# Layer 0's neighbour sums for seven row blocks from two float32r pieces, and an 8-bit mask read directly

## The chip, the cores and the metric

The kernel runs on one core of a Trainium2 chip. The metric is the device time of one execution in microseconds, as the median over repeated executions. The engines are PE (TensorE, matmuls), DVE (VectorE), ACT (ScalarE), POOL (GpSimd, here mostly the gathers) and SP (SyncE, which issues the other transfers).

## The reference

Four graph layers follow each other on a matrix x of 3327 rows and 512 columns, each with a residual and a layer norm, over one sparse 0/1 adjacency. The change lies in layer 0, a graph attention layer with 8 heads of 64 columns:

```python
Wh = einsum('nd,hdo->hno', x, W)
f1 = einsum('hno,ho->hn', Wh, a1);  f2 = einsum('hno,ho->hn', Wh, a2)
e  = leaky_relu(f1[:, :, None] + f2[:, None, :], 0.2)
e  = where(adj > 0, e, -9e15)
h  = einsum('hnm,hmo->hno', softmax(e), Wh)
x  = layernorm(x + elu(h))
```

Layer 1 sums masked neighbours and multiplies by dense weights, layer 2 does so over the first 64 neighbours of a row, layer 3 is another attention layer with 4 heads.

## The kernel before

The 3327 rows are 26 blocks of 128. A first stage, `structure`, reads the adjacency block by block and makes, for every block but block 0, a list of its edges (`EdgeList`). Density falls with the row number, so the lists get shorter: in chunks of 128 edges they hold 19, 15, 13, 11, 10, 9 for blocks 1 to 6, then 9, 8, 8, 8, 7, 7, 7 for blocks 7 to 13, and 7 down to 5 for blocks 14 to 25. Block 0 is dense and is not done by a list.

`projection` writes the rows of Wh with their scores, 8 heads of 66 columns (528 in all), into a table in DRAM. Then, per block, `groups` cuts the list into groups of at most `GROUP = 4` chunks, and `Gat.group` does a group in stages (each `yield` ends one). Line numbers are those of the profile:

- POOL gathers 528-column rows of the table into the ring tile `gt` (line 973); ACT computes `far` (1206), DVE from it the selector `ds` (1210).
- PE brings the rows' own scores to the edges (1218) and turns the selector (1224). DVE adds the scores (1228, 1229), ACT takes two exponentials (1230, 1231) and copies the turned selector out of PSUM into `sel` (1233).
- DVE multiplies the gathered rows by their weights in place (1238).
- PE adds `sel`-transposed times rows into two accumulators of 264 columns, in float32 (1249), chunk by chunk.

When a block's last chunk is in, `layer0_end` divides by head (1361 to 1365, ACT does 8 divisions), does ELU and layer norm (1375 to 1378, 789, 791, and on POOL the root, 799 and 800; `nm` 843 and the scaled row 844), turns the result (769, 772) and multiplies it by two weights of layer 1 (784), whose results go to DRAM in two pieces (1546, 1547) or as they are (1554). For this, steps of an earlier block stand between the steps of the groups.

Block 0 is done densely beside the last seven lists: `open_dense` makes a factor per head, and `dense` takes one block of 128 table rows after another (`gd`, loaded on SP), scales them by ACT (1315, eight heads), makes a weight matrix of 8 x 128 columns by DVE (1316, 1317), which is masked by block 0's adjacency, and adds the product (1324). That mask is kept as `row0` in 8-bit floats; ACT first copies it into a float32 tile `mk` with two buffers (1306), which line 1317 reads.

Up to and including layer 0 the instructions stand in the order that the scheduler of the language gives them when the kernel is built; from layer 1 on they stand as written. Every engine runs its queue in order. Tiles come from pools with a fixed number of buffers: a write into a tile waits until the last reader of the earlier tile in that buffer has ended.

Of the kernel before, what the change touches and what calls it, by code (L numbers as in the profile page):

```python
# [8 lines left out]
F32 = mybir.dt.float32  # L9
BF16 = mybir.dt.bfloat16  # L10
FP8 = mybir.dt.float8e4
F32R = mybir.dt.float32r
# [5 lines left out]
AF = mybir.ActivationFunctionType  # L18
# [5 lines left out]
P = 128  # L24
# [509 lines left out]
GROUP = 4  # L534
# [6 lines left out]

FIRST = 1
DENSE = 7
RING = 22 * 528
MORE = 3072
RANGE = 60.0
# [29 lines left out]
class Ring:  # L576
# [20 lines left out]
    def done(self):  # L597

        self.live.pop(0)
# [28 lines left out]
def sparse_path(ctx, tc, flag_i, x, adj, l0_w, l0_a1, l0_a2, l1_w_self, l1_b_self, l1_w_nb, l1_b_nb,  # L628
# [13 lines left out]
    nc = tc.nc  # L642
    N, D = x.shape
    NB = (N + P - 1) // P
# [10 lines left out]
    def pool_in(lay, name, bufs=1, **kw):  # L655
        return lay.enter_context(tc.tile_pool(name=name, bufs=bufs, reuse_waits="tile", **kw))
# [17 lines left out]
    chunks_of = [sum(l.L for l in ls) for ls in lists]  # L674
# [67 lines left out]
    H0, _, OUT0 = l0_w.shape  # L742
# [207 lines left out]
                                                   ALU.is_gt, ALU.mult)  # L950
            yield k

    def groups(ring, blocks=range(NB)):


        for b in blocks:
            at = 0
            for l in lists[b]:
                c0 = 0
                while c0 < l.L:  # L960
                    left = l.L - c0
                    g = -(-left // -(-left // GROUP))
                    if ring.ahead() < g:
                        g = ring.ahead()
                    yield b, l, c0, g, at
                    c0 += g
                    at += g
# [26 lines left out]
    class Gat:  # L994
# [197 lines left out]
        def group(self, item, pools, accs, done, sall=None):  # L1192

            b, l, c0, g, at = item
            ring, sp, pacc, pone = pools
            H, OUT, M = self.H, self.OUT, self.M
            hh = H // 2
            G = gather(ring, self.table, l, c0, g)

            m = l.places(c0 + g - 1)  # L1200
            for p0 in range(m, P, 32):
                nc.scalar.copy(G[p0:p0 + 32, g - 1].rearrange("p (h m) -> p h m", m=M)[:, :, OUT:],
                               zeros[p0:p0 + 32, :2 * H].rearrange("p (h s) -> p h s", s=2))

            far = sp.tile([P, GROUP * P], I16, name="far")
            nc.scalar.activation(far[:, :g * P], place[:, c0 * P:(c0 + g) * P], AF.Abs, bias=l.nmid, scale=2.0)
            yield
            have = kept(sall, b, at, g)
            ds = sp.tile([P, GROUP * P], BF16, name="ds")
            nc.vector.tensor_scalar(ds[:, :g * P], far[:, :g * P], dgs[:, l.at:l.at + 1], None, ALU.is_lt)  # L1210
            yield

            pg = pone.tile([P, 512], F32, name="pg")
            pe = pg[:, :GROUP * 2 * H].rearrange("p (c s h) -> p c s h", c=GROUP, s=2)
            w = pg[:, GROUP * 2 * H:GROUP * 3 * H].rearrange("p (c h) -> p c h", c=GROUP)
            for c in range(g):
                for k in range(3):
                    nc.tensor.matmul(pe[:, c], ds[:, c * P:(c + 1) * P], self.own[:, k, :, b],
                                     start=k == 0, stop=k == 2)
            S = sp.tile([P, GROUP, P], F32, name="sel")  # L1220
            if have is None:
                turned = pg[:, 256:].bitcast(BF16)
                for c in range(g):
                    nc.tensor.transpose(turned[:, c * P:(c + 1) * P], ds[:, c * P:(c + 1) * P], ident16)
            yield
            sc = sp.tile([P, GROUP, 2, H], F32, name="sc")
            Gh = G.rearrange("p c (h m) -> p c h m", m=M)
            nc.vector.tensor_tensor(sc[:, :g], pe[:, :g], Gh[:, :, :, OUT:].rearrange("p c h s -> p c s h"), ALU.add)
            nc.vector.tensor_tensor(sc[:, :g, 0], sc[:, :g, 0], sc[:, :g, 1], ALU.max)
            nc.scalar.activation(w[:, :g], sc[:, :g, 0], AF.Exp)  # L1230
            nc.scalar.activation(Gh[:, :, :, OUT], sc[:, :g, 0], AF.Exp)  # L1231
            if have is None:
                nc.scalar.copy(S[:, :g], turned[:, :g * P].rearrange("p (c i) -> p c i", i=P))  # L1233
            else:
                nc.scalar.activation(S[:, :g], have, AF.Identity)
            yield
            Gc = G.rearrange("p c (h m) -> p (c h) m", m=M)
            nc.vector.tensor_mul(Gc[:, :, :OUT], Gc[:, :, :OUT],  # L1238
                                 w[:, :g].rearrange("p c (h o) -> p (c h) o", o=1).to_broadcast([P, g * H, OUT]))
            yield  # L1240
            while self.held[self.turn] if at == 0 else b not in accs:
                yield
            if at == 0:
                accs[b] = self.sums(pacc, self.turn)
                self.turn ^= not self.pinned
            for c in range(g):
                m = l.places(c0 + c)
                for s in range(2):
                    nc.tensor.matmul(accs[b][s], S[:m, c, :], G[:m, c, s * hh * M:(s + 1) * hh * M],  # L1249
                                     start=at + c == 0, stop=at + c == chunks_of[b] - 1)  # L1250
            ring.done()
            if at + g == chunks_of[b]:
                done(b, accs.pop(b))

        def sums(self, pacc, turn):

# [37 lines left out]
        def dense(self, j, pool, ps, pacc, done):  # L1294
# [7 lines left out]
            gd, wt = self.gd[j % 3], self.wt[j % 2]  # L1302
            for p0, p1 in rows_of(j):
                nc.sync.dma_start(gd[p0:p1], self.table[2 + j * P + p0:2 + j * P + p1, :])
            mask = pool.tile([P, P], F32, name="mk", bufs=2)
            nc.scalar.activation(mask, row0[:, j, :], AF.Identity)
            yield
            g = gd.rearrange("p (h m) -> p h m", m=M)
            fs = pool.tile([P, 2, H], F32, name="fs", bufs=2)
# [4 lines left out]
            for h in range(H):  # L1314
                nc.scalar.activation(g[:m, h, :OUT], g[:m, h, :OUT], AF.Identity, scale=g[:m, h, OUT:OUT + 1])
            nc.vector.tensor_tensor(wt[:m], self.up[:m], fs[:m, 1, :, None].to_broadcast([m, H, P]), ALU.max)
            nc.vector.tensor_mul(wt[:m], wt[:m], mask[:m, None, :].to_broadcast([m, H, P]))
            yield

            def out(h):  # L1320
# [238 lines left out]
    def transposed_weights():  # L1559

        n = len(raws) - 2
        jobs = [(src, o, k) for src, o in ((l2_w_nb, wn2), (l2_w_line, wl2)) for k in range(DC)]

        def fetch(i):
            src, _, k = jobs[i]
            nc.sync.dma_start(raws[i % n], src[k * P:(k + 1) * P, :])

        for i in range(n):
            fetch(i)
        yield  # L1570
        for i, (_, o, k) in enumerate(jobs):
            yield
            pt = ps.tile([P, DC, P], F32, name="pt", tag="tr")
            for c in range(DC):
                nc.tensor.transpose(pt[:, c, :], raws[i % n][:, c * P:(c + 1) * P], ident)
            nc.scalar.copy(o[:, :, k * P:(k + 1) * P], pt)
            if i + n < len(jobs):
                fetch(i + n)

    w2lay, dlay = ExitStack(), ExitStack()  # L1580
    def feed():

        left = list(range(NB))
        blocks = [b for b in order if b]
        for n, b in enumerate(blocks):
            if n == len(blocks) - DENSE - 2:
                assert wn2 is not None
                dp = pool_in(dlay, "l0d")
                work.add(g0.open_dense(fin, ps, pools[2], dp.tile([P, H0 * P], F32, name="up"),
                                       *[raws[-1 - k] for k in range(2)],  # L1590
                                       *[dp.tile([P, H0 * g0.M], F32, name=f"gd{k}") for k in range(3)]))
            for item in groups(pools[0], (b,)):
                yield item
                for _ in range(2):
                    if left and n >= len(blocks) - DENSE:
                        yield left.pop(0)
        yield from left

    for k, item in enumerate(feed()):
        if isinstance(item, int):  # L1600
            work.add(g0.dense(item, fin, ps, pools[2], layer0))
        else:
            while ready < order.index(item[0]):
                more()
            work.add(g0.group(item, pools, accs, layer0))
        work.step()
        more(2)
        if ready == NB - 1 and wn2 is None:
            listlay.close()
            aside = pool_in(ctx, "s_more")  # L1610
            wp = pool_in(w2lay, "l2w")
            wn2 = wp.tile([P, DC, D], F32, name="wn2")
            wl2 = wp.tile([P, DC, D], F32, name="wl2")
            places = aside.tile([P, MORE], F32, name="raw", tag="aside")
            raws = [places[:, k * D:(k + 1) * D] for k in range(2)]
            raws += [places[:, (k + 1) * H0 * P:(k + 2) * H0 * P] for k in range(2)]
            work.add(transposed_weights())
    ps = Banks(ps, acc0=pools[2])
    ps.shared = dict(po="acc0")
# [376 lines left out]
```

## Time and profile before

| | |
|---|---|
| median of 8 runs | 1724.51 us (1721.97 to 1731.35) |
| the profiled execution | 1719.89 us, span 1718.2 us |
| PE, PE's weight loads | busy 1515.5 us (88%), 1010.1 us (59%) |
| DVE, ACT, POOL | 1194.8 us (70%), 821.1 us (48%), 858.7 us (50%) |
| granted PE clock, mean | 0.951 |
| line 1249, layer 0 (rows `gt`) | 804 matmuls from 226.7 to 670.0 us, 386 ns median each |

A recorded matmul's duration holds its way through the array, which the next one overlaps; what a stream of them costs is read from the distance of their starts. A float32 matmul of the kernel stands in the trace as two instructions. The busy share of the whole span says little, since the stages have different bounds: the text reads each stage by itself.

### The profile page before, as it was taken

What the parts mean: (1) busy time and instruction counts of PE and PEld (TensorE: products, weight loads), DVE (VectorE), ACT (ScalarE), POOL (GpSimd) and SP (SyncE); (2) the same over time, 40 slices, a digit from 0 to 9 for tenths busy, and PEclk for the clock granted to TensorE, in tenths of its full rate; (3) what the DMA queues carried; (4) which work ended last, traced back from release to release, by engine and by line L of the source; (5) the groups of instructions that cost most, each with busy time, mean ns of one, the idle gap of its engine ahead of it and who ended that gap; (6) DMA issues with size and microseconds to landing.
All of it is one profiled execution on the core that took longest, in us unless ns stands there. A gap on an engine that the chain in (4) does not pass through costs nothing.

```text
span 1718.2 us, 24775 instructions
## 1 busy us (share of the span) xinstructions
PE 1515.5 (88%) x7729; PEld 1010.1 (59%) x7729; DVE 1194.8 (70%) x2887; ACT 821.1 (48%) x2728; POOL 858.7 (50%) x936
## 2 busy tenths in 40 slices
PE   5899868999999998899999998768999987698774
PEld 4666656666666675355555554324666765577653
DVE  8987889975578795046566676566666545788986
ACT  4887856675557685121212111203444443465664
POOL 2000076655545300566555653177777706777770
PEclk9899978999999999889999999999999998899997
DMA  8787688766555531899999998288999916777772
GB/s 288 231 290 249 195 301 283 233 211 196 175 162 167 166 97 44 296 376 344 297 349 330 350 395 290 88 294 285 306 321 316 325 39 170 213 230 224 229 223 71
DMA packets 127073, 414.45 MB, mean 241 GB/s; under 512 B 23299, under 2 KB 24835, under 8 KB 126932
## 3 DMA queue, kind: packets, MB, share of 16 engines
q0 software_dynamic: 78128, 293.23, 52.7%
q1 hardware_dynamic: 48804, 119.55, 20.0%
q8 instruction: 63, 1.03, 0.2%
q14 instruction: 78, 0.64, 0.1%
HBM read 364.40 MB, written 48.30 MB: 240 GB/s over the span
## 4 chain that ended last, share of the span: by engine, by line
PE 42%; DVE 7%; DMA 7%; ACT 5%; issue 3%; POOL 2%; DVEq 0%; POOLq 0%; ACTq 0%
PE po L784 14%; PE acc L1681 11%; PE acc L1249 5%; PE po L1010 5%; DMA gl<-t_d,idx 3%; PE pt L769 2%; DMA gm<-t_d,idx 2%; PE acc L1175 1%; DMA gk<-t_d,idx 1%; POOL gl L973 1%; DVE gl L1238 1%; ACT h L1365 1%; DVE st L789 1%; PE acct L1324 1%; PE acc L1757 1%
## 5 line engine op out<-in xcount | busy, mean ns | idle before, releaser
L973 POOL DMA_INDIRECT gl<-t_d,idx x334 | 330.7, 990 | 197.1 <-issue 137.5
L973 POOL DMA_INDIRECT gt<-t_d,idx x201 | 201.2, 1001 | 333.4 <-DVE g0fall L832 201.3
L973 POOL DMA_INDIRECT gm<-t_d,idx x159 | 158.5, 997 | 115.8 <-PE acc L1681 62.5
L1249 PE MATMUL acc<-gt,sel 128*128 128x264 f32 (+3 forms) x804 | 207.1, 405 | 1.5 <-issue 1.4
L1249 PE MATMUL acc<-gl,sel 128*128 128x260 f32 (+3 forms) x684 | 176.6, 410 | 32.8 <-issue 24.0
L784 PE MATMUL po<-wn,xt 128*128 128x512 f32 x416 | 195.1, 612 | 9.7 <-ACT xt L772 5.7
L1249 PEld LDWEIGHTS acc<-gt,sel 128*128 128x128 f32 (+3 forms) x804 | 151.5, 197 | 39.3 <-issue 14.9
L1249 PEld LDWEIGHTS acc<-gl,sel 128*128 128x128 f32 (+3 forms) x684 | 132.3, 201 | 59.2 <-issue 29.4
L784 PEld LDWEIGHTS po<-wn,xt 128*128 128x128 f32 x416 | 79.0, 196 | 93.9 <-issue 77.0
L1681 PE MATMUL acc<-gm,selr 128*128 128x512 f32 (+2 forms) x360 | 119.8, 464 | 9.4 <-DMA gm<-t_d,idx 6.7
L1238 DVE TENSOR_TENSOR gt<-gt,pg 128x1536 f32<-128x1536 f32 (+3 forms) x63 | 116.5, 1849 | 14.1 <-ACT sel L1233 13.8
L1010 PE MATMUL po<-gt,xt 128*128 128x268 f32 x416 | 109.3, 410 | 8.9 <-ACT xt L776 5.7
L772 ACT COPY xt<-pt 128x512 f32<-128x512 f32 x81 | 47.4, 592 | 135.6 <-PE pt L769 125.8
L892 DVE MAX8 cand<-val 128x8 f32<-128x464 uint16 (+32 forms) x184 | 106.1, 619 | 0.0
L769 PE MATMUL pt<-s_ident,xres 128*128 128x128 f32 x500 | 77.4, 282 | 30.2 <-DMA xres<-in_x_dram 16.3
L1238 DVE TENSOR_TENSOR gl<-gl,pg 128x1536 f32<-128x1536 f32 (+3 forms) x53 | 98.2, 1852 | 2.2 <-ACT gl L1231 2.0
L1010 PE MATMUL po<-w,xt 128*128 128x262 f32 x416 | 98.6, 390 | 0.5 <-ACT xt L776 0.5
L784 PE MATMUL po<-wx,xt 128*128 128x512 f32 x208 | 95.4, 604 | 0.4 <-DVE t L1547 0.4
L1681 PEld LDWEIGHTS acc<-gm,selr 128*128 128x128 f32 (+2 forms) x360 | 67.5, 201 | 47.1 <-issue 18.5
L1010 PEld LDWEIGHTS po<-gt,xt 128*128 128x128 f32 x416 | 77.9, 196 | 28.5 <-ACT xt L776 7.8
L868 ACT ACTIVATE m<-ab 128x1664 bf16<-128x1664 int32 x50 | 81.1, 1624 | 27.1 <-DMA ab<-in_adj_dram 18.8
L784 PE MATMUL po<-wl,xt 128*128 128x512 f32 x208 | 93.1, 593 | 0.0
(334 smaller groups left out, 3063.8 us busy)
## 6 DMA issues: line engine op xcount, KB each, us to landing
ab<-in_adj_dram SPq DMA_DIRECT2D x25, 832.0 KB, 6.8
ab<-in_adj_dram SPq DMA_DIRECT2D x25, 831.5 KB, 6.2
t_d<-t SPq DMA_DIRECT2D x25, 512.0 KB, 3.2
gm<-t_d POOLq DMA_DIRECT2D x20, 512.0 KB, 9.5
t_d<-t SPq DMA_DIRECT2D x25, 384.0 KB, 6.7
t_d<-tg SPq DMA_DIRECT2D x25, 264.0 KB, 4.9
gd<-t_d SPq DMA_DIRECT2D x25, 264.0 KB, 3.3
t_d<-tg SPq DMA_DIRECT2D x25, 260.0 KB, 5.2
```

What stands on the lines that cost most here:

```text
L769: nc.tensor.transpose(pt[:, c, :], src[:, c * P:(c + 1) * P], ident)
L772: nc.scalar.copy(xt, pt)
L784: nc.tensor.matmul(po, xt[:, c, :], w[:, c], start=c == 0, stop=c == DC - 1)
L789: nc.vector.bn_stats(st, y)
L868: nc.scalar.activation(m, ab[s], AF.Sign, accum_out=half[:, s, b:b + 1])
L892: nc.vector.max(out=cand[:, s, :], in_=val[:, cuts[s]:cuts[s + 1]])
L973: nc.gpsimd.indirect_dma_start(out=t[:m, c, :], out_offset=None, in_=table[:, :], in_offset=bass.IndirectOffsetOnAxis(ap=l.idx[:m, c0 + c: ...
L1010: nc.tensor.matmul(pw[s], xt[:, c, :], self.w[:, c, s, :], start=c == 0, stop=c == DC - 1)
L1175: nc.tensor.matmul(self.acc[h // hh][:, h % hh, :], wt[:m, h, :], G[:m, h, :], start=False, stop=False)
L1238: nc.vector.tensor_mul(Gc[:, :, :OUT], Gc[:, :, :OUT], w[:, :g].rearrange("p c (h o) -> p (c h) o", o=1).to_broadcast([P, g * H, OUT]))
L1249: nc.tensor.matmul(accs[b][s], S[:m, c, :], G[:m, c, s * hh * M:(s + 1) * hh * M], start=at + c == 0, stop=at + c == chunks_of[b] - 1)
L1681: nc.tensor.matmul(accs[b], chosen, parts[:, k * D:(k + 1) * D], start=at + c + k == 0, stop=k == top and at + c == n - 1)
```

## The change

In blocks 7 to 13 of layer 0 (`PARTED`) a group has at most 3 chunks. After the product of line 1238, ACT copies the group's rows into a float32r tile `hi`, and DVE subtracts that from the rows into a second one, `lo`; both are halves of one tile `hl` with a single buffer. `sel` is float32r in these blocks. PE then adds `sel` times `hi` and `sel` times `lo` instead of one float32 product. The pool that held the dense block's `up` and three `gd` tiles is opened earlier, when the structure stage ends, and has one buffer, which first holds `hl` and then, as `room0`, those four. Line 1317 reads `row0` itself; `mk` and its copy are gone.

```diff
+PARTED = range(7, 14)
+THREE = 3
...
-    def groups(ring, blocks=range(NB)):
+    def groups(ring, blocks=range(NB), most=lambda b: GROUP):
...
-                    g = -(-left // -(-left // GROUP))
+                    g = -(-left // -(-left // most(b)))
...
-            S = sp.tile([P, GROUP, P], F32, name="sel")
+            split = self.k == 0 and b in PARTED
+            S = sp.tile([P, GROUP, P], F32R if split else F32, name="sel" + "r" * split, tag="sel")
...
-            yield
+            if split:
+                hi, lo = self.parts()
+                nc.scalar.copy(hi[:, :g], G)
+            yield
+            if split:
+                nc.vector.tensor_sub(lo[:, :g], G, hi[:, :g].bitcast(F32))
...
+                parts = (hi, lo) if split else (G,)
                 for s in range(2):
-                    nc.tensor.matmul(accs[b][s], S[:m, c, :], G[:m, c, s * hh * M:(s + 1) * hh * M],
-                                     start=at + c == 0, stop=at + c == chunks_of[b] - 1)
+                    for k, part in enumerate(parts):
+                        nc.tensor.matmul(accs[b][s], S[:m, c, :], part[:m, c, s * hh * M:(s + 1) * hh * M],
+                                         start=at + c + k == 0,
+                                         stop=at + c == chunks_of[b] - 1 and k == len(parts) - 1)
...
+        def parts(self):
+            hl = self.dp.tile([P, 2, THREE, self.H * self.M], F32R, name="hl", tag="d")
+            return hl[:, 0], hl[:, 1]
...
-            mask = pool.tile([P, P], F32, name="mk", bufs=2)
-            nc.scalar.activation(mask, row0[:, j, :], AF.Identity)
...
-            nc.vector.tensor_mul(wt[:m], wt[:m], mask[:m, None, :].to_broadcast([m, H, P]))
+            nc.vector.tensor_mul(wt[:m], wt[:m], row0[:m, j, None, :].to_broadcast([m, H, P]))
...
-                dp = pool_in(dlay, "l0d")
-                work.add(g0.open_dense(fin, ps, pools[2], dp.tile([P, H0 * P], F32, name="up"),
-                                       *[raws[-1 - k] for k in range(2)],
-                                       *[dp.tile([P, H0 * g0.M], F32, name=f"gd{k}") for k in range(3)]))
-            for item in groups(pools[0], (b,)):
+                room0 = g0.dp.tile([P, 2 * THREE * H0 * g0.M], F32, name="room0", tag="d")
+                gds = [room0[:, H0 * P + k * H0 * g0.M:][:, :H0 * g0.M] for k in range(3)]
+                work.add(g0.open_dense(fin, ps, pools[2], room0[:, :H0 * P], *[raws[-1 - k] for k in range(2)],
+                                       *gds))
+            for item in groups(pools[0], (b,), lambda b: THREE if b in PARTED else GROUP):
...
+            g0.dp = pool_in(dlay, "l0d")
             work.add(transposed_weights())
```

## The prediction

> **What bounds the kernel now.** I read the page first (its slices show PE at 9 tenths in slices 9 to 12 while DVE and ACT stand at 4 to 7), then the order of the work on PE to find where blocks 7 to 13 lie. Line 1249 runs 4 recorded matmuls a chunk (two column halves, each float32 product in two passes), blocks 1 to 6 have 77 chunks and blocks 7 to 13 have 54, so the blocks of the change are its instructions 309 to 524; counted through the stages, they stand at 362 to 472 us. The busy times by stage:
>
> ```profile
> core 0: us, PE busy (x) PEld busy (x) DVE busy (x) ACT busy (x) POOL busy (x), PEclk, DMA share, GB/s
> 362.00:472.00 110.00, 109.02 (x604) 74.44 (x603) 66.00 (x148) 65.65 (x197) 59.23 (x72) 1.00 0.64 195
> 215.00:362.00 147.00, 121.96 (x834) 89.10 (x831) 134.63 (x371) 90.18 (x257) 100.63 (x104) 0.88 0.81 262
> 520.00:600.00 80.00, 74.94 (x459) 56.17 (x458) 62.49 (x109) 58.37 (x221) 38.63 (x39) 1.00 0.54 166
> 600.00:660.00 60.00, 57.81 (x396) 46.15 (x396) 53.87 (x95) 49.08 (x200) 5.77 (x6) 1.00 0.29 92
> ```
>
> From 362 to 472 PE is the bound, with 1 us idle in 110, and DVE and ACT have 44 us free each. In the stage before, DVE is the bound (92%). So the matmuls that the change shortens are on the path. PE's order of time inside it:
>
> ```profile
> 435.11 3.73 PE L1249 MATMUL acc<-gt,sel 128*128 128x264 f32 x16
> 438.68 0.44 PE L1218 MATMUL pg<-g0own,ds 128*128 128x16 bf16 x9
> 438.95 0.33 PE L1224 MATMUL pg<-ident,ds 128*128 128x128 bf16 x3
> 439.12 3.65 PE L784 MATMUL po<-wn,xt 128*128 128x512 f32 x8
> ```
>
> Sixteen instructions from 435.11 to 438.68 are 0.223 us each; a chunk costs 0.89 us, blocks 7 to 13 cost 216 x 0.223 = 48.2 us, and the other 61 us are scores, transposes and the dense products that end earlier blocks.
>
> **The matmuls.** The count stays 4 a chunk (two halves, two pieces), each now one float32r pass of 264 columns. No such pass is in the trace; the nearest are layer 1's, 512 wide, beside bfloat16 ones of that width:
>
> ```profile
> 855.61 1.63 PE L1681 MATMUL acc<-gm,selr 128*128 128x512 f32 x6
> 857.08 3.60 PE L784 MATMUL po<-wx,xt 128*128 128x512 f32 x8
> ...
> 878.36 0.82 PE L1757 MATMUL acc<-t,near 128*128 128x512 bf16 x3
> 879.02 0.60 PE L769 MATMUL pt<-s_ident,xres 128*128 128x128 f32 x4
> ```
>
> Six float32r passes take 1.47 us, 0.245 each; bfloat16 takes 0.66/3 = 0.220. Half the float32 pitch is 0.111. Scaled by width, 0.245 gives 0.126; with the 30 ns by which it exceeds 512 columns at 0.111 per 264 (0.215) kept as a fixed cost, 0.141. I take 0.141, as the pass loads the same float32r selector, with 0.111 below and no gain (0.223) above. PE saves 216 x (0.223 - 0.141) = 17.7 us (24.2 to 0) and needs about 91 us. That the selector is written as float32r costs nothing: it is the same ACT copy out of PSUM, off the bound today.
>
> The Trainium skill speaks against this edit: its page "TensorE: Matmul & The Clock Gate", sections "LDWEIGHTS" and "Weight-path perf modes", gives a load of 128 weight columns 1/1.2 ns each, and its fast load not for float32. By that an unhidden load of 107 ns would stand beside a pass of about 110, and the saving would be about 1 us, the forecast then near rival 3's. Here four transposes, each with a float32 load of 128 columns, start and end within 0.44 us (0.11 each), so such loads do overlap, but no run here shows one under a float32r pass this short.
>
> **The pieces.** Groups in these blocks go from at most 4 chunks to at most 3: 15 groups become 21, 12 of three and 9 of two. Each adds one ACT copy and one DVE subtraction of 528 elements a chunk. Their prices:
>
> ```profile
> L830 ACT CAST t<-tb x26: 606/619/622, 757.6 to 1099.3; 128x512 bf16<-128x512 f32 x26
> L830 ACT CAST g0own<-g0fall x1: 539/539/539, 209.9 to 209.9; 128x416 bf16<-128x416 f32 x1
> ...
> L1238 DVE TENSOR_TENSOR gt<-gt,pg 128x2048 f32<-128x2048 f32 x8 | 18.3, 2284 | 5.7 <-ACT sel L1233 5.7
> L1238 DVE TENSOR_TENSOR gt<-gt,pg 128x1536 f32<-128x1536 f32 x4 | 7.0, 1753 | 0.3 <-ACT sel L1233 0.3
> L1238 DVE TENSOR_TENSOR gt<-gt,pg 128x1024 f32<-128x1024 f32 x3 | 3.7, 1217 | 0.0
> ```
>
> ACT: 0.833 ns an element, so 1.51 us for 1584 and 1.07 for 1056, in all 12 x 1.51 + 9 x 1.07 = 27.8 us. DVE: 1.04 ns, so 1.80 and 1.25, in all 32.9 us. Six more groups bring six more fixed parts: 0.63 us on DVE (what product, scores and selector have at zero width) and 0.86 on ACT, 3.8 and 5.1 us. Off this stage go some 2 us of DVE and 4.2 of ACT: two dense blocks that are prepared early, whose space is now the pieces' (their three loads on SP wait for the pieces; t1 stores stand behind them, which have time until layer 1). The stage then holds DVE 100.7, ACT 94.4, PE 91 us. The bound moves to DVE, with ACT close, and only 9 us below the 110.
>
> **The wait it adds.** The pieces' tile has one buffer. So the copy of one group waits until PE has ended the group before; on ACT's queue the exponentials, selector copies and head divisions stand behind it, and on DVE the next product and scores stand behind each subtraction. I walked block 9 (groups A, B of three, C of two) along the queues of the changed program with the row prices, in us: copy A 0 to 1.5, subtraction A 1.6 to 3.4, PE's 12 matmuls free the tile at 5.3. DVE meanwhile does the product of B (to 5.1), an ending's subtraction and the product of C (to 7.0). ACT has 4.2 us of its other work, so copy B is 5.8 to 7.3, subtraction B 7.4 to 9.2; PE, busy with 3.4 us of line 784, sums B from 9.4 and frees the tile at 11.3. Copy C waits for that, to 12.4; DVE has scores and a layer norm until 13.7, subtraction C to 15.0, the next product to 16.8, where the next copy starts. Before, 8 chunks took 8 x 110/54 = 16.3. Block 11 (7 chunks) walks to 14.7 against 14.3. So 3% longer: +3.3 us on 110.
>
> Two things that the walk leaves out. PE will have gaps; stages with gaps show granted clocks of 0.88 and 0.92 to 0.96. At 0.92 the 216 x 0.141 = 30.5 us of piece matmuls grow by 2.7, at 0.88 by 4.2. And a layer norm's nm, which stands ahead of one subtraction in each block, waits for POOL's rs: 13.1 us in 7 waits now, where the walk gave 0.6 each; a quarter of the other 8.9, +2. Bounds of both together: 0 and 13.
>
> **The mask from 8 bits.** 26 ACT copies go (0.2 us each between starts, 5.2 us), and their wait for the buffer:
>
> ```profile
> L1306 ACT ACTIVATE mk<-row x26: 292/309/364, 217.3 to 646.7; 128x128 f32<-128x128 fp8e4 x26
> its engine sat idle before it (us, times) until:
>   DVE raw L1317: 9.3, 8
> ```
>
> That is ACT time from 472 to 660, where PE is 95% busy: it idles 7.3 us from 520 to 660, some 5.2 of them behind ACT. So the gain is 0 to 7.3; I take half of ACT's 5.2: -2.5; late next there are the eight scalings of a dense block (line 1315, 1.8 us a block), on the same queue. DVE's product of 1024 keeps its 1.22 us, bounded by no row with an 8-bit operand on DVE.
>
> **Sum.** +3.3 + 2.7 + 2.0 - 2.5 = +5.5 us. The profiled execution took 1719.9 (span 1718.2 and 1.7 around it) and lies 4.6 below the median of the runs, 1724.5; the difference is put on the median: 1730.
>
> **Rivals.** 1. The queues pack: DVE fills its stage without gaps, 100.7 us, as it came to 92% in the stage before (which would be 109). Against it: ACT at 94% of such a stage and the single buffer; for it: the copies of the order are interleaved with other work. The stage loses 9, the mask 2.5: 1713. It decides once ACT's copy mostly finds the tile free. With PE still the bound it would be 1724.5 - 17.7 - 2.5 = 1704.3, which I hold for unlikely, since DVE alone needs more. 2. Break-even: stage and mask cancel, within 0.2%, which is 3.4 us and about what a measurement of this kernel tells from no change: 1724. 3. The float32r pass saves nothing (the change doesn't do what it says): the piece matmuls, behind each subtraction, last 0.082 x 12 or x 8 longer, 12 x 0.98 + 9 x 0.66 = 17.7 us more on the walk's path: 1747.
>
> **How the numbers follow.** Slower as summed 0.40, rival 3 0.10, break-even 0.18, faster (rival 1) 0.32. The range for 8 in 10 reaches down to rival 1's 1713, and up to 1743: the sum with the bound of clock and waits (13 in place of 4.7), half of the mask's gain lost (1.2) and the walk's 3% doubled (3.3). That leaves rival 3 out, and part of the faster case's low tail, where PE stays the bound.
>
> **What would show it.** In the profile after: the stage of blocks 7 to 13 at 108 to 122 us with DVE over 85% busy, PE near 80%; a pitch of 0.13 to 0.15 on the new matmuls; copies waiting for PE, PE waiting for the subtraction. Wrong if the stage is under 105 us, if the copy or subtraction of 1584 is far from 1.5 and 1.8 us, or if the dense stage, 472 to 660, moves by over 6 us.

## The result and the profile after

The changed kernel takes 1731.97 us (median of 20 runs, 1727.22 to 1738.37) against 1724.63 for the kernel before (57 runs): a ratio of 1.0044, 95% interval [1.0032, 1.0055], 7.3 us slower where 5.5 were forecast. The two profiled executions have spans of 1729.4 and 1718.2 us. That of before lies 4.6 us under its median, so differences between single profiles come out some 4 us larger than those between medians, and the text says which of the two it uses.

The stage of blocks 7 to 13 moved as a whole. The busy times by stage, of the profile after (columns as in the prediction; the last but two is the granted clock):

```profile
core 0: us, PE busy (x) PEld busy (x) DVE busy (x) ACT busy (x) POOL busy (x), PEclk, DMA share, GB/s
215.00:362.00 147.00, 122.39 (x795) 89.35 (x795) 132.08 (x365) 87.21 (x250) 99.83 (x103) 0.87 0.79 257
362.00:472.00 110.00, 97.09 (x586) 62.01 (x584) 91.06 (x174) 82.27 (x201) 61.98 (x67) 0.97 0.61 184
369.00:482.00 113.00, 98.03 (x597) 64.08 (x595) 92.66 (x174) 84.31 (x208) 63.47 (x68) 0.93 0.61 185
520.00:600.00 80.00, 73.92 (x451) 54.96 (x450) 58.64 (x110) 53.96 (x191) 40.38 (x42) 1.00 0.59 179
600.00:660.00 60.00, 56.42 (x397) 45.39 (x398) 55.45 (x96) 48.83 (x200) 8.19 (x8) 1.00 0.31 90
```

PE, which had 1 us idle in 110, has 13 there now. The stage itself runs from 368.8 to 482.2 us (third row) where it ran from 369.0 to 474.8: 113.4 us for 105.8, with 15 us of PE idle and a clock of 0.93. A second ruler needs no counting of matmuls: the start is the first of DVE's eight small scalings (line 1276, after the change 1292), the end PE's first product of line 1280 (1296), which the next stage begins with. The groups of tile `raw`, first of before, then of after:

```profile
L1276 DVE TENSOR_SCALAR raw<-s_ident,f1c x8: 256/279/304, 361.4 to 364.8; 128x128 f32<-128x128 f32 x8
L1280 PE MATMUL pf<-raw,s_ones x4: 592/620/697, 490.3 to 500.0; 128*128 128x512 f32 x4
```

```profile
L1292 DVE TENSOR_SCALAR raw<-s_ident,f1c x8: 231/278/405, 361.7 to 371.2; 128x128 f32<-128x128 f32 x8
L1296 PE MATMUL pf<-raw,s_ones x4: 592/620/697, 497.8 to 505.5; 128*128 128x512 f32 x4
```

So this stretch, called **the stretch** below, takes 128.9 us before and 136.1 after, +7.2. Each stretch is read from one profile; two profiles of one later program gave 123.3 twice.

What the new matmuls cost is read from the distance of starts on PE, in the profile after:

```profile
387.81 1.71 PE L1259 MATMUL acc<-hl,selr 128*128 128x264 f32 x12
389.43 0.44 PE L1220 MATMUL pg<-g0own,ds 128*128 128x16 bf16 x9
...
390.20 3.60 PE L786 MATMUL po<-wx,xt 128*128 128x512 f32 x8
393.64 0.27 PE L1589 MATMUL pt<-s_ident,raw 128*128 128x128 f32 x1
393.67 1.70 PE L1259 MATMUL acc<-hl,selr 128*128 128x264 f32 x12
395.21 0.44 PE L1220 MATMUL pg<-g0own,ds 128*128 128x16 bf16 x9
```

Twelve in 1.62 and 1.54 us are 0.135 and 0.128 each, against 0.223 for the float32 instructions they replace. The saving is there. It is given back between the groups; the last two of the stage:

```profile
462.21 3.57 PE L786 MATMUL po<-wn,xt 128*128 128x512 f32 x4
465.62 0.34 PE L1220 MATMUL pg<-g0own,ds 128*128 128x16 bf16 x6
...
471.13 0.51 PE L1259 MATMUL acc<-hl,selr 128*128 128x264 f32 x2 [1.16 <-ACT hl L1245]
472.43 1.69 PE L1259 MATMUL acc<-hl,selr 128*128 128x264 f32 x6 [0.79 <-DVE hl L1248]
```

Here PE stands idle for the copy and then for the subtraction, and four instructions of a dense product take 3.41 us, where eight such ones took 3.44 in block 8 (390.20 to 393.64 above): PE runs at half speed here. The trace records the clock as 0.50 from 462.2 to 465.6 us and from 472.4 to 486.1, and once more from 434.9 to 438.3. By tens of us:

```profile
440.00:450.00 10.00, 7.62 (x48) 4.64 (x47) 7.63 (x10) 9.38 (x23) 4.50 (x5) 1.00 0.57 165
450.00:460.00 10.00, 8.89 (x56) 5.57 (x54) 7.91 (x20) 7.01 (x21) 6.32 (x7) 1.00 0.55 161
460.00:470.00 10.00, 9.11 (x52) 5.43 (x52) 9.08 (x15) 5.00 (x11) 4.08 (x6) 0.83 0.50 140
470.00:480.00 10.00, 6.45 (x40) 5.04 (x41) 8.07 (x15) 7.89 (x21) 5.77 (x6) 0.62 0.53 166
480.00:490.00 10.00, 10.00 (x29) 6.31 (x28) 4.36 (x13) 4.68 (x17) 3.80 (x5) 0.70 0.56 162
```

Not every gap is followed by a halved clock: the longest of the stage, 2.1 us before 415.96 behind a subtraction, is not. Tile by tile, the two new steps and what they meet:

```profile
L1245 ACT CAST hl<-gt x21: 1071/1512/1587, 362.5 to 474.7; 128x1584 fp32r<-128x1584 f32 x12, 128x1056 fp32r<-128x1056 f32 x9
L1248 DVE TENSOR_TENSOR hl<-gt,hl x21: 1249/1801/1809, 364.2 to 477.0; 128x1584 fp32r<-128x1584 f32 x12, 128x1056 fp32r<-128x1056 f32 x9
its engine sat idle before it (us, times) until:
  ACT hl L1245: 20.1, 28
  DVE hl L1248: 13.8, 15
  issue: 4.5, 18
  PE acc L1259: 3.5, 5
```

The first two rows of the list are idle time of PE (sums and weight loads) and of DVE behind ACT's copy, and of PE behind DVE's subtraction. The last row is the wait for the single buffer: ACT stood idle for it 3.5 us in all. The waits of the whole stage (368 to 482 us) say the same and add who else is behind; five of the rows:

```profile
POOL gt L975 <- DVE hl L1248: 27.2, 12, 3.6
DVE hl L1248 <- ACT hl L1245: 8.0, 9, 2.5
PE acc L1259 <- DVE hl L1248: 5.5, 6, 2.1
DVE nm L845 <- POOL rs L802: 5.0, 3, 2.8
PE acc L1259 <- ACT hl L1245: 4.5, 8, 1.2
```

The gathers now wait for DVE's subtraction, which is the last to read the ring, where they waited 21.8 us for PE's sums before. The layer norm's `nm` waits 5.0 us, not more than before (11.7 in six waits in the same window).

The mask's copy is gone, and its operand costs DVE nothing extra:

```profile
L1331 DVE TENSOR_TENSOR raw<-raw,row x26: 1194/1221/1226, 511.0 to 662.2; 128x1024 f32<-128x1024 f32 x25, 127x1024 f32<-127x1024 f32 x1
```

The first dense matmul came 6.7 us late (514.8 to 521.5) and the last 8.5 (660.8 to 669.3): the dense stage gave nothing back and took 1.8 us more itself.

### The profile page after: what moved, and what is told of

The parts are those of the page before. It is cut to its first block, busy times and chain, and to the rows that moved or that the text cites. A ratio compares the mean times of both kernels' runs of the same rounds, so it can differ in the third digit from the quotient of the medians.

```text
span 1729.4 us, 24788 instructions
## 1 busy us (share of the span) xinstructions
PE 1515.0 (88%) x7729; PEld 1005.4 (58%) x7729; DVE 1223.2 (71%) x2924; ACT 842.1 (49%) x2739; POOL 865.4 (50%) x936
## 4 chain that ended last, share of the span: by engine, by line
PE 42%; DVE 7%; DMA 6%; ACT 4%; issue 3%; POOL 2%; DVEq 0%; POOLq 0%; ACTq 0%
PE po L786 14%; PE acc L1696 11%; PE acc L1259 7%; PE po L1012 5%; DMA gl<-t_d,idx 3%; PE pt L771 2%; DMA gk<-t_d,idx 1%; PE acc L1177 1%; POOL gl L975 1%; DMA gm<-t_d,idx 1%; DVE gl L1241 1%; DVE st L791 1%; ACT h L1379 1%; PE acc L1772 1%; PE acct L1338 1%
## 5 line engine op out<-in xcount | busy, mean ns | idle before, releaser
L975 POOL DMA_INDIRECT gt<-t_d,idx x201 | 206.0, 1025 | 343.7 <-DVE cand L894 200.3
L786 PE MATMUL po<-wn,xt 128*128 128x512 f32 x416 | 201.7, 625 | 8.8 <-ACT xt L774 5.9
L1259 PE MATMUL acc<-gt,sel 128*128 128x264 f32 (+3 forms) x588 | 159.4, 418 | 2.2 <-issue 2.2
L1259 PEld LDWEIGHTS acc<-gt,sel 128*128 128x128 f32 (+3 forms) x588 | 113.5, 203 | 30.7 <-issue 12.0
L1241 DVE TENSOR_TENSOR gt<-gt,pg 128x1536 f32<-128x1536 f32 (+2 forms) x67 | 117.0, 1747 | 8.1 <-ACT sel L1236 7.2
```

Source lines behind the costliest of these rows:

```text
L786: nc.tensor.matmul(po, xt[:, c, :], w[:, c], start=c == 0, stop=c == DC - 1)
L975: nc.gpsimd.indirect_dma_start(out=t[:m, c, :], out_offset=None, in_=table[:, :], in_offset=bass.IndirectOffsetOnAxis(ap=l.idx[:m, c0 + c: ...
L1241: nc.vector.tensor_mul(Gc[:, :, :OUT], Gc[:, :, :OUT], w[:, :g].rearrange("p c (h o) -> p (c h) o", o=1).to_broadcast([P, g * H, OUT]))
L1259: nc.tensor.matmul(accs[b][s], S[:m, c, :], part[:m, c, s * hh * M:(s + 1) * hh * M], start=at + c + k == 0, stop=at + c == chunks_of[b] - ...
```

## The experiments

The runs of this section are from three chips. The kernel before took 1724.61 us on the first, 1854.17 on the second (with a mean clock of 0.92 where it is 0.95 on the first; what else makes it slow there is not known) and 1724.21 on the third; every ratio is to the runs of before on the same chip. Theories at the start: A, the chain copy, subtraction, sums on DVE's full queue makes PE idle; rivals, that the smaller groups, the single buffer or the mask do it.

**The mask alone.** The kernel before, with `row0` read directly.

```diff
-            mask = pool.tile([P, P], F32, name="mk", bufs=2)
-            nc.scalar.activation(mask, row0[:, j, :], AF.Identity)
...
-            nc.vector.tensor_mul(wt[:m], wt[:m], mask[:m, None, :].to_broadcast([m, H, P]))
+            nc.vector.tensor_mul(wt[:m], wt[:m], row0[:m, j, None, :].to_broadcast([m, H, P]))
```

> The kernel before with line 1317 reading the 8-bit mask and the copy gone, nothing else. Theory A (the copy stood in ACT time that no one waited for): within 2 us of before. Theory B (my prediction's term): 2.5 us faster, up to 7.

Measured: 1729.59 us, 1.0027 [1.0006, 1.0049]: 5.0 us above before, so no gain, and more likely a loss of 1 to 8 us; theory A's 2 us lie near the interval's end, theory B's gain outside it. ACT's copy had waited 9.3 us for DVE before; the waits of ACT from 510 to 665 us without it, in this run:

```profile
ACT fs L1309 <- DVE fs L1308: 10.8, 10, 2.9
ACT pg L1230 <- DVE sc L1229: 9.2, 7, 1.8
```

The first stood at 6.5 us before, the second at 0.8 (one wait). ACT waits for the same DVE a few instructions later: the wait moved. The matmuls of the dense block last 145.6 us (512.1 to 657.7) against 146.0.

**Groups of three alone.** Blocks 7 to 13 in groups of at most 3 chunks, float32 sums as before.

```diff
-    def groups(ring, blocks=range(NB)):
+    def groups(ring, blocks=range(NB), most=lambda b: GROUP):
...
-                    g = -(-left // -(-left // GROUP))
+                    g = -(-left // -(-left // most(b)))
...
-            for item in groups(pools[0], (b,)):
+            for item in groups(pools[0], (b,), lambda b: 3 if 7 <= b < 14 else GROUP):
```

> The kernel before with groups of at most three chunks in blocks 7 to 13, float32 sums as before, no pieces. Theory A (DVE and ACT have 44 us free in the stage, six more groups bring 4 and 5 us): within 2 us of before. Rival (the smaller groups are what costs): 5 us or more slower.

Measured: 1721.91 us, 0.9989 [0.9970, 1.0008]; the stretch 127.8 us. The six more groups are not what costs.

**No subtraction.** The changed kernel without DVE's subtraction; PE adds `hi` twice, so the low piece is left out of the sum.

```diff
-            if split:
-                nc.vector.tensor_sub(lo[:, :g], G, hi[:, :g].bitcast(F32))
...
-                parts = (hi, lo) if split else (G,)
+                parts = (hi, hi) if split else (G,)
```

> The changed kernel without DVE's subtraction: both passes on PE read the high piece, so the low piece is left out of the sums and counted wrongly. PE and ACT have the same work, DVE has 33 us less. Theory A (DVE with its subtraction sets the stage): the stage falls from 113 to 95 to 102 us, the time to 1718 to 1723, under before. Rival (the copy behind the single buffer, or PE's lowered clock, sets it whatever DVE does): 1728 to 1732.

Measured: 1718.55 us, 0.9961 [0.9937, 0.9984], 13 us under the changed kernel; the stretch 120.6 us, and the stage itself, from 370.9 to 469.9 us, 99 where theory A gave 95 to 102. In the tens of us from 430 to 490 the clock stays at 1.00, and PE is busy 9.3 to 9.6 of each (earlier in the stage it was halved twice, for 3.4 us from 400.2 and from 417.2). The copies and the single tile are all still there; the subtraction (with the wait it adds) is what turns the gain into a loss.

**Every other block.** The changed kernel with pieces in blocks 8, 10 and 12 alone, once on the first chip and again on the third.

```diff
-PARTED = range(7, 14)
+PARTED = (8, 10, 12)
```

> The changed kernel with pieces in blocks 8, 10 and 12 alone, 24 of the 54 chunks. PE saves 24 x 4 x 0.09 = 8.6 us, DVE gets 16 us more on 66. Theory A (the loss comes when DVE and ACT have no room left): PE keeps work from the blocks between, 3 to 7 us faster than before. Rival (each block of pieces costs by its chain copy, subtraction, sum): 0 to 4 us slower than before.

> The every-other kernel (blocks 8, 10 and 12 in pieces, 8-bit factors) once more, to see whether its gain holds on this chip: ratio 0.994 to 0.998 if it does, 0.999 to 1.001 if the first measurement was luck of the clock.

Measured: 1717.64 us, 0.9958 [0.9932, 0.9983], and again 1720.46 us, 0.9976 [0.9961, 0.9991]; the stretch 123.3 us both times. It beats both kernels. The stage in the second of the two, and the gathers' wait for the subtraction:

```profile
362.00:472.00 110.00, 106.75 (x633) 71.99 (x632) 82.12 (x169) 77.92 (x219) 67.01 (x73) 1.00 0.69 206
```

```profile
POOL gt L975 <- DVE hl L1248: 8.8, 3, 3.9
```

PE is idle 3 us of the 110 where the changed kernel has 13, the clock is 1.00, DVE has 28 us free, and in the waits of PE's matmuls neither piece appears (its weight loads wait 1.4 us for them). A block of float32 sums behind each pieced one leaves PE with work while DVE catches up; that is the reading of these rows, and no run shows it by itself.

**The changed kernel again**, on the second chip, as the measure for the next two.

> The changed kernel once more, unchanged, for a second profile beside the next kernels. Theory A (the last two blocks of pieces lose their time to a lowered PE clock that follows from PE's gaps): the clock of 430 to 475 us is again under 0.95, where the kernel before had 1.00, and the time 5 to 9 us above before. Rival (the dip was chance): 1.00 there, and the stage 4 to 5 us shorter.

Measured: 1873.61 us, 1.0104 [1.0078, 1.0130]; the stretch 145.3 us, the gathers' wait for the subtraction 37.1 us (396 to 520). The clock from 430 to 475 us is 0.92, as theory A expected (the stage lies some 30 us later there). The loss is there on this chip too, and larger than its 5 to 9 us: 19.4.

**Tiles of their own.** `hi` and `lo` in a tile each, PE adding all `hi` of a group first, so that `hi` comes free earlier, without waiting for the subtraction and the sums of `lo`. The dense block's four factors move into the two tiles (not shown).

```diff
-            hl = self.dp.tile([P, 2, THREE, self.H * self.M], F32R, name="hl", tag="d")
-            return hl[:, 0], hl[:, 1]
+            return [self.dp.tile([P, THREE, self.H * self.M], F32R, name=n, tag=t)
+                    for n, t in (("hi", "d"), ("lo", "dl"))]
...
-            for c in range(g):
-                m = l.places(c0 + c)
-                parts = (hi, lo) if split else (G,)
-                for s in range(2):
-                    for k, part in enumerate(parts):
+            parts = (hi, lo) if split else (G,)
+            for k, part in enumerate(parts):
+                for c in range(g):
+                    m = l.places(c0 + c)
+                    for s in range(2):
```

> The changed kernel with the high and the low piece in two tiles, each with a buffer of its own, and PE summing all high pieces of a group before the low ones: the next copy then waits only for the high half of the sums and the subtraction. The four dense factors lie in the two tiles. Theory A (DVE's own work sets the stage; ACT waited only 3.5 us for the buffer): 0 to 3 us faster than the changed kernel. Rival (the single buffer makes the loss): 5 to 10 us faster than the changed kernel.

Measured: 1864.21 us, 1.0058 [1.0036, 1.0079]: 9.4 us less than the changed kernel on the same chip (by the two intervals, some 2 to 15); the stretch 133.6 us for 145.3, and

```profile
POOL gt L975 <- DVE lo L1248: 19.4, 11, 3.2
```

So the single buffer and the order of the sums make a good part of the loss, though ACT's direct wait for the tile was short (3.5 us on the first chip): they also hold back PE's first passes until the subtraction is done, which the order of this kernel doesn't. Which of the two it is, this run doesn't separate. A second buffer for `hl` was not tried.

**The odd blocks**, 7, 9, 11 and 13 (`PARTED = (7, 9, 11, 13)`).

> Pieces in blocks 7, 9, 11 and 13, 31 of the 54 chunks. DVE gets 21 us on 66, PE saves 11 of 109. Theory A (blocks of pieces and of float32 side by side fill both engines): as every other block, 5 to 9 us faster than before. Rival (the three of 8, 10, 12 were chance, or block 13 with its end at the low clock loses its share): 0 to 3 us faster.

Measured: 1866.75 us, 1.0071 [1.0048, 1.0093]: slower by 12.6 us where both expectations had a gain. The stretch is 137.8 us, better than the changed kernel's 145.3; against the every-other kernel that follows, on the same chip, it is 5.7 us longer there and 9.0 us longer behind it. Those two kernels differ in three things: which blocks, how many (31 chunks for 24) and the mask's copy. So this run doesn't show which of them decides.

**Every other block with the mask's copy kept**, in one bfloat16 buffer.

```diff
-PARTED = range(7, 14)
+PARTED = (8, 10, 12)
...
+            mask = pool.tile([P, P], BF16, name="mk")
+            nc.scalar.activation(mask, row0[:, j, :], AF.Identity)
...
-            nc.vector.tensor_mul(wt[:m], wt[:m], row0[:m, j, None, :].to_broadcast([m, H, P]))
+            nc.vector.tensor_mul(wt[:m], wt[:m], mask[:m, None, :].to_broadcast([m, H, P]))
```

> Pieces in blocks 8, 10 and 12, and the mask copied by ACT as before, but into one bfloat16 buffer in place of two of float32. Theory A (the direct mask is worth nothing or costs a little, as run alone): 0 to 4 us faster than the same with the direct mask. Theory B (my term of -2.5): 2 to 3 us slower than that.

Measured: 1849.91 us, 0.9978 [0.9961, 0.9994]; the stretch 132.1 us. So three pieced blocks gain with the mask's copy kept as well. Which of the two theories on the mask is right stays open, as the every-other kernel with the direct mask did not run on this chip; its ratios on the others, 0.9958 and 0.9976, have intervals that overlap with this one's.

**The last block alone, and all but the last.** Block 13 had looked like the place of the loss in the profile after (5 of the 7.4 us, at half clock). `PARTED = (13,)` and `PARTED = range(7, 13)`, both on the third chip:

> The changed kernel, but only block 13, the last of the stage, is summed from the two pieces; blocks 7 to 12 as before; the 8-bit factors stay. Theory L (the loss sits in the last block, where there is no next list of the same stage to put between subtraction and sums, and the granted clock fell to 0.60): 2 to 5 us slower than before, ratio 1.001 to 1.003, and its clock row near the end of the stage shows the dip. Theory A (every pieced block costs the same, through DVE): a seventh of the whole, under 1 us, ratio 0.9995 to 1.001.

> The counterpart: blocks 7 to 12 from the two pieces, block 13 as before, 8-bit factors kept. Theory L: without the last block the loss is gone or nearly so, ratio 0.999 to 1.001, stage end at most 3 us later than before's. Theory A: six sevenths of the whole loss remain, ratio 1.004 to 1.006.

Measured: 1726.09 us, 1.0012 [0.9998, 1.0026], and 1728.31 us, 1.0028 [1.0011, 1.0044]. The first lies in theory L's range, and its interval overlaps with theory A's as well; the dip in clock that L expected near the stage's end isn't there (1.00 in each ten us from 430 to 490). Theory L's number for all but the last, 0.999 to 1.001, is missed, since more than half of the loss remains; theory A's 1.004 to 1.006 lies at the upper edge of the interval. In the profiles the stretch is no longer than before's in either (128.7 and 127.1 us): by them the last block costs it out of proportion only behind six others, and what these two kernels lose stands behind the stretch. The stage of all but the last has the same shape, milder, with the dip in clock elsewhere (0.90 and 0.93 from 440 to 460 us, 1.00 after):

```profile
362.00:472.00 110.00, 99.14 (x579) 63.95 (x579) 91.39 (x183) 83.46 (x212) 60.31 (x66) 0.98 0.65 196
```

```profile
POOL gt L975 <- DVE hl L1248: 24.0, 11, 4.1
```

**Both improvements.** Tiles of their own, pieces in 8, 10 and 12.

> Blocks 8, 10 and 12 alone in pieces, with the two pieces in tiles of their own and all first passes ahead of all second ones. If both gains add (every other block gave 0.9958, tiles of their own took 9.4 us off the changed kernel), ratio 0.990 to 0.995. If the gap between the pieced blocks already frees the single buffer in time, the same as the every-other kernel, 0.994 to 0.998.

Measured: 1721.01 us, 0.9982 [0.9965, 1.0000]; the stretch 122.9 us. The gains don't add. In the every-other kernel the copies waited only 1.2 us for the single buffer (368 to 482 us, second run), so there was little left to gain from it.

The stretch of all kernels side by side, and the next one, from its end to the first sum over `gm` rows, which layer 1 begins with (dense stage and last lists):

| kernel | ratio | the stretch, us | the next, us |
|---|---|---|---|
| before | 1 | 128.9 | 217.4 |
| changed | 1.0044 | 136.1 | 220.4 |
| mask alone | 1.0027 | 128.9 | 220.3 |
| groups of three (copy kept) | 0.9989 | 127.8 | 218.7 |
| no subtraction | 0.9961 | 120.6 | 222.7 |
| every other, twice | 0.9958, 0.9976 | 123.3, 123.3 | 222.8, 219.9 |
| last alone | 1.0012 | 128.7 | 221.9 |
| all but last | 1.0028 | 127.1 | 222.9 |
| every other, own tiles | 0.9982 | 122.9 | 220.3 |
| second chip: changed | 1.0104 | 145.3 | 228.1 |
| second chip: own tiles | 1.0058 | 133.6 | 228.6 |
| second chip: odd blocks | 1.0071 | 137.8 | 230.0 |
| second chip: every other, copy kept | 0.9978 | 132.1 | 221.0 |

The first column of times is what the pieces do: 5.6 us gained with three blocks, 1.8 with six, 7.2 lost with seven, 8.3 gained with seven without the subtraction. The second column hints at an effect that was not foreseen: on the first and third chip the kernels that read the factors from 8 bits have 219.9 to 222.9, the two that copy them 217.4 and 218.7; on the second 228.1 to 230.0 for 221.0. One program profiled twice differs there by 2.9 us, so no single pair of rows shows it. What carries more weight is the mask alone: 5.0 us slower by its median, with nothing else changed.

## Why the prediction was right, and where its steps were not

The direction, the time (1730.0 for 1731.97) and the stage were right. Step by step:

- **The matmuls.** Forecast 0.141 us a pass. The groups of ten and twelve that run at full clock take 0.13 to 0.17 a pass from their first start to the next instruction, and inside a group the median distance of two starts is 0.12, nearer to the 0.126 that the forecast scaled by width. At the halved clock it is 0.25 (six in 1.49 us from 472.43). The float32 weight load of 107 ns that the prediction, taking it as unhidden, held against the edit (the Trainium skill, "TensorE: Matmul & The Clock Gate", section "LDWEIGHTS") does not show beside a pass: passes that each load their own selector start 0.128 and 0.135 us apart on average in the two groups of twelve above, and the page's 0.107 on top of a pass of 0.11 would be, as an estimate, 0.217. Rival 3 is out.
- **Copies and subtractions.** 18.2 + 9.8 us on ACT, 21.7 + 11.3 on DVE; forecast 27.8 and 32.9. Right.
- **The bound.** "The bound moves to DVE" was right in effect, since the run without the subtraction takes it away, but not as a full engine. DVE is 82% busy in the stage (92.7 of 113), not over 85, and PE 87%, not 80. The forecast's sums of 100.7 and 94.4 us for DVE and ACT came out at 92.7 and 84.3. Some 3 to 4 us of each come from the place where it looked: before, the blocks' sums ran from 369.0 to 474.8 us, not 362 to 472, and there DVE had 63.0 us and ACT 62.0, not 66.0 and 65.7. The rest may be other lists' work that moved behind the stage's end; that was not counted.
- **The walk.** From a block's first copy to the next block's it gave 16.8 us for block 9 and 14.7 for block 11; the profile after has 17.7 (399.9 to 417.6) and 15.7 (433.1 to 448.7), a stretch of halved clock included in the second. Blocks 7 to 12 together took 2.4 us more than before (their sums end at 462.4 for 460.0), near the share that they have in the 3.3. The last block alone took another 5, with PE idle and at half clock, and the walk had nothing for that. The copies that wait for the buffer, the wait that the walk was made for, come to 3.5 us in all; that the buffer and the order of the sums cost more than this shows only in the kernel with tiles of their own.
- **The clock** was the term that was mis-sized. The price of 2.7 us put a clock of 0.92 on the 30.5 us of piece matmuls only. The clock was 0.93, but it slows everything that PE does in the stage: of its 98.0 us, 7% are 6.9, an estimate that is not all added to the stage. The dense products show it without any change of their own; PE's groups from 369 us to the stage's end, after and then before (mean ns in the column before the last bar):

```profile
L786 PE MATMUL po<-wn,xt 128*128 128x512 f32 x49 | 25.4, 638 | 0.4 <-ACT xt L774 0.4
L786 PE MATMUL po<-wx,xt 128*128 128x512 f32 x48 | 23.7, 627 | 1.8 <-DVE t L1561 1.8
```

```profile
L784 PE MATMUL po<-wn,xt 128*128 128x512 f32 x49 | 22.4, 598 | 0.0
L784 PE MATMUL po<-wx,xt 128*128 128x512 f32 x48 | 21.9, 598 | 0.0
```

  These 97 instructions alone hold 4.8 us more. From first to last sum PE's busy time fell by 6.4 us (104.8 to 98.4) where the forecast had 17.7 less in matmuls, and 14.0 us of idle time came in: that is the 7.6 by which the stage is longer (113.4 for 105.8).
- **The wait of `nm`**, +2.0, was wrong: 5.0 us in the stage now, 11.7 before.
- **The mask**, -2.5, was wrong in sign or worth nothing. The step that failed counted ACT's wait at the copy as time that would go. It was a wait for DVE, and ACT meets DVE again at the next instruction in line. That the 8-bit operand costs DVE no more was right (1.22 us). Of the signs of being wrong, "the dense stage moves by over 6 us" came true only as a shift: its first matmul came 6.7 us late, and its length changed by 1.8.
- **Rival 1**, the queues that pack, is not what the changed kernel did; the version with three pieced blocks, at 1717.6 and 1720.5, is the nearest to it, where it gave 1713 for seven.

So the nearness of the sum is luck in part. Its three terms for the stage come to 8.0 us and the stage grew by 7.6 in the profiles, but the clock was priced at 2.7 for up to 6.9, and the 2.0 of `nm` were not there. Without the 2.5 that the mask was to give, the forecast would have been 8.0 for the measured 7.3. As terms, the prices and the pitch held, and the walk roughly, 1 us too short in each of its two blocks; clock, `nm` and mask did not.

**What stays open.** How the 7.3 us divide between pieces and mask: in the profiles the stretch of the pieces takes 7.2 more, yet by the medians the mask alone is 5.0 slower and the changed kernel only 2.4 above that. The mask alone measured 1 to 8 us, and its intervals with the kernels of one block (-0.3 to 4.5) and six blocks (1.9 to 7.6), which hold the mask too, overlap widely. Why the kernel is slower without the copy: the dense matmuls of the mask alone take no longer, DVE's product costs the same, and what its profile has more, 3.3 us, lies behind the last dense matmul; where the profiles differ is the clock, at another place in each (the mask alone has 0.73 from 660 to 685 us where before has 0.86; on the second chip the changed kernel has 0.88 from 520 to 560 where the every-other kernel with the copy has 1.00). That this is a cause is not shown. What makes the clock fall: PE idles before each of the three halved stretches, but also where it stays full. Why blocks 7, 9, 11 and 13 lose while 8, 10 and 12 gain: the last block's 2.1 us explains a part at most, and the direct mask may explain another. Seven pieced blocks with the copy kept were not tried.

## What to carry to other kernels

Splitting an operand so that the bounding engine does less is worth only what the helpers' slack can carry in order: three blocks of seven fit into DVE's and ACT's free time and gained 4 to 7 us (four of seven, measured only on the second chip and with the direct mask, lost), while all seven made a chain that idled the engine they were to relieve. Price gaps on PE twice, once as idle time and once as lower clock on all that it does nearby. A copy that is seen waiting need not be a cost: ask which wait the queue meets next.

## What the runs showed of the hardware

A float32r pass of 264 columns with its own float32r weight load starts 0.12 us after the one before (median inside a group), though the load itself is recorded with 188 ns. A float32 product of DVE with an 8-bit factor takes what one with a float32 factor does (1.22 us for 1024). PE's granted clock was halved for stretches of 3.4 and 13.7 us in a stage where PE was 87% busy and no gap was longer than 2.1 us, and it stayed at 1.00 with 0.4 to 0.7 us of gaps in ten (no subtraction, 430 to 490 us). The share of idle time alone doesn't tell when: from 440 to 450 us PE was busy 7.6 of 10, and the clock was 1.00 there and in the ten behind; from 470 to 480 it was busy 6.5, at 0.62, and the ten us behind, busy throughout, still had 0.70. And the same program took 1724 us on two chips and 1854 on a third; the changed kernel was slower than before both times that the two were compared, and the kernels with blocks 8, 10 and 12 were faster on all three.
